# Last stage of a four-layer Flamingo block: values of two head pairs at a time, and other work moved between the slots

## The chip, the cores and the metric

The kernel runs on one core of one Trainium2 chip. The metric is device time in microseconds of one execution; three executions of the kernel before took 1777.65, 1778.09 and 1778.33 us, median 1778.09.

The engines of the core run side by side, each with its own instruction queue in order: TensorE (PE, matmuls; PEld are its weight loads), VectorE (DVE), ScalarE (ACT), GpSimd (POOL) and SyncE (SP, which here only issues DMAs). They meet through semaphores. Matmul results lie in PSUM[...].

## The reference

There are four layers on a batch of 16 sequences of 256 tokens, 256 channels each: a cross attention, a mixture of experts, a second cross attention, and a gated linear attention with a dense and a routed part. The change touches the last layer alone. Cut to what matters:

```python
q1 = (x @ Wq).reshape(B, L, H, DK) * scale;  k1 = (x @ Wk).reshape(B, L, H, DK)
v  = (x @ Wv).reshape(B, L, H, DV)
q2 = (x @ Wqa @ Wqb) * scale;  k2 = softmax(x @ Wka @ Wkb)          # per head
gk1 = log_sigmoid(x @ Wg1a @ Wg1b + bg1) / 16;  gk2 = ...           # decays
e = softmax(x @ We);  _, idx = top_k(e, 1);  mask = one_hot(idx)    # routing, 4 experts
o_dense  = gla(q1, k1, v, gk1)
o_sparse = sum over experts of gla(q2 * e * mask, k2 * e * mask, v, gk2 * mask)
o = o_dense + o_sparse
g = x @ Wga @ Wgb                                                    # output gate
o = o * rsqrt(mean(o * o) + EPS) * norm_w * (g * sigmoid(g))         # per head
x = x + tanh(g_ffn[1]) * (o.reshape(B, L, H * DV) @ Wo)
```

Here `x` is the normalised input (layer norm), H = 8 heads of 64, and `gla` is a causal linear attention with decays.

## The kernel before

`stage3_fast` computes the last layer. Its loop at the end runs over p = 4 b + m: b is the batch (0 to 15), m the pair of heads (0 to 3). I call the four steps of a batch its **slots 0 to 3**. All engines keep the program's order in this stage. What a slot does is written out in the loop, together with tables (`middle`, `rest`, `late`, `behind_factors`, `by_rows`, `logs`), which say by p % 4 which step runs at which place of the slot, and for which batch (an offset to b).

For each head pair, in this order through slots p-1 to p+1:

- `keys_queries` (bank `kq`): keys and queries, 4 matmuls, 8 records in the profile (each fp32 matmul gives two).
- `decays` (banks `gq`, `gz`): sums of the log gates along the tokens for the dense and the routed part, then four exps on ACT (`ee`).
- `factors` on DVE (`f`): keys and queries of the dense part times the exps. `second` and `factors_second`: keys and queries of the routed part (`k` on POOL, `q` on DVE).
- `products(p, 0)` and `products(p, 1)`: scores of the dense and the routed part (`sc`, `sc1`). The two heads of a pair lie in two row tiles of 64.
- `masked(p, 0)` (`at` on DVE), `masked(p, 1)` (four scalar_tensor_tensor instructions on DVE, then the sum of both parts by POOL's `at<-at,at`).
- `values`: the summed scores times `v`, into the bank `o`, two column tiles of 64. `summed(p)` calls it for p-1, and at even p also `squares` (ACT). `gated` multiplies `o` by the output gate `gw` into `u` (DVE).

Once for each batch:

- `lows` in slot 0 (the narrow projections), for the next batch. `all_gates` and `gates_end` in slot 1: exps of the gates into `lg`; `gate_logs` later turns them into logs.
- Routing: `route_logits`, `route_sums` and `route` (DVE, 32x32 tiles). `route` ends with SP's DMA `picks<-chosen` to memory and two DMAs back: `rows<-picks` (spread over the partitions) and `cols<-picks`. `same` (`em`) and `weights` (`am`), on DVE, build masks from both.
- Output gate: `outgates` in slot 0, `outgates_copy` (`zs`), and `outgates_end` for each of two halves: two ACT instructions on `eg`, then POOL's `gw<-zs,eg`.
- `stats`, `norm_ahead` (`xn`) and `turn_ahead` for the batch after next: the layer norm, and its transposition by DVE and by 16 SP DMAs `xnT<-turned`, which `lows` of that batch needs.
- `norms` in slot 1 for the batch before: sums of squares (bank `ms`), `rs` on ACT, SP's DMA `rms<-rs` to memory and two DMAs `r<-rms` back; `normed_out` (POOL, two `u<-u,r`), then `project` in slot 3: 16 records `proj<-wo,u`, the residual on DVE and the output DMA.

SP issues its DMAs in the program's order: in a batch `lowd`, `low`, then `picks`, `rows`, `cols`, `rms`, two `r`, sixteen `xnT`, `out`.

Tiles with the same tag share buffers in turn. In `f3w2` each tag has two. The tag `zs` serves both halves of the output gate and `rows`:

```python
x = w2.tile([P, 512], F32, tag="zs", name="rows") if b else ...     # route, line 1760
e, zs = (w2.tile([P, 512], F32, tag=n, name=n) for n in ("eg", "zs"))   # outgates
```

`bank(...)` gives one of two general PSUM banks in turn. `psa` is one pair of banks for scores (`sc`), also used by `all_gates`; `kq`, `gq`, `gz` and `o` have a bank each.

Of the kernel before, what the change touches and what calls it, by code (L numbers as in the profile page):

```python
# [10 lines left out]
F32 = mybir.dt.float32  # L11
I32 = mybir.dt.int32
AF = mybir.ActivationFunctionType
# [60 lines left out]
def layers(ctx: ExitStack, tc: tile.TileContext, t, out, check):  # L74
# [1559 lines left out]
    def stage3_fast(early_bank):  # L1634

        with ExitStack() as sx:
# [7 lines left out]
            def bank(name):  # L1644
                return pss.tile([P, 512], F32, tag="ps", name=name) if pss else early_bank(name)
# [129 lines left out]
            def all_gates(b):  # L1775

                lg[b] = of(b).tile([P, 2, 2, 512], F32, tag="lg", name="lg")
                two = psa.tile([P, 2, 512], F32, tag="sc", name="sc")
                one = [bank("z"), bank("z")]
                for i in (1, 0):  # L1780
                    for n, (lo, hi) in enumerate(((0, 17), (32, 49))):
                        x, w = (low2[lo:hi, :], lbg2[lo:hi, :]) if i else (low[b][64 + lo:64 + hi, 1, tokens(0)],
                                                                         lbg[64 + lo:64 + hi, :])
                        matmul(two[:, n, :] if i else one[n], x, w, start=True, stop=True)
                act3.activation(lg[b][:, 0, 0, :], one[0], AF.Exp, scale=-1.0)
                act3.activation(lg[b][:, 1], two, AF.Exp, scale=-1.0)
                z_[b, "z"] = one[1]

            def gates_end(b):
                act3.activation(lg[b][:, 0, 1, :], z_.pop((b, "z")), AF.Exp, scale=-1.0)  # L1790

            def gate_logs(b, i):
                act3.activation(lg[b][:, i], lg[b][:, i], AF.Ln, bias=1.0)
# [136 lines left out]
            def products(p, n):  # L1930

                b, m, cols = place(p)
                q, k = fq.pop((p, n)), fk.pop((p, n))
                if p == last - 1 and n == 1:
                    two = [psu.tile([P, 512], F32, tag=x, name="sc1") for x in ("kq", "gq")]
                elif n == 1 and m > 1:
                    two = [bank("sc1"), bank("sc1")]
                else:
                    ps = z_[p, n, "sc"] = psa.tile([P, 2, 512], F32, tag="sc", name="sc")
                    two = [ps[:, 0, :], ps[:, 1, :]]  # L1940
                for lo, hi, i in ((0, S, 0), (P, S, 1)):
                    for j in range(2):
                        r = slice(64 * j, 64 * j + 64)
                        matmul(two[j][:, lo + i * P:hi + i * P], k[r, tokens(i)], q[r, lo:hi],
                                         start=True, stop=True)
                if n == 1:
                    z_[p, n, "sc"] = two

            def masked(p, n):
                b, m, cols = place(p)  # L1950
                ps = z_.pop((p, n, "sc"))
                a = w2.tile([P, 2, 384], F32, tag=f"at{n}", name=f"at{n}")
                if n == 0:
                    at[p] = a
                    dve3.tensor_tensor(a, ps[:, :, :384], bc(amask, [P, 2, 384], 1), ALU.mult)
                else:
                    r = rd[b][:, 2 * m:2 * m + 2, :]
                    parts = [(j, 0, S, 0) for j in range(2)] + [(j, S, 3 * P, 1) for j in range(2)]
                    for j, lo, hi, i in parts if p == last - 1 else sorted(parts):
                        dve3.scalar_tensor_tensor(a[:, j, lo:hi], ps[j][:, lo:hi], r[:, i, j:j + 1],  # L1960
                                                  am[b][:, lo:hi], ALU.mult, ALU.mult)
                    if p == last - 1:
                        at[p, 1] = a
                        return
                    pool3.tensor_tensor(at[p], at[p], a, ALU.add)

            def values(p, first=True, end=True):
                b, m, cols = place(p)
# [13 lines left out]
            def squares(b, mp):  # L1982
                if mp == 0:
                    u_[b] = w2.tile([P, 4, S], F32, tag="u", name="u")
                    oT[b] = u_[b]
                    sq[b] = w2.tile([P, 4, S], F32, tag="sq", name="sq")
                ps = o.pop((b, mp))
                act3.activation(sq[b][:, 2 * mp:2 * mp + 2, :].rearrange("p m s -> p (m s)"), ps, AF.Square)
                z_[b, mp, "o"] = ps
# [17 lines left out]

            rms = [tc.dram_tile([8, S], F32, name=f"rms{b}") for b in range(B - 1)]

            def scaled_first(b):  # L2010
                if b == B - 1:
                    scaled(b, 0)

            def norms(b):

                if b == B - 1:
                    return
                ps, x = bank("ms"), sq.pop(b)
                for m in range(4):
                    matmul(ps[32 * m:32 * m + 32, :S], halves[:, 48:80], x[:, m, :], start=True, stop=True)  # L2020
                y = w2.tile([P, S], F32, tag="rs", name="rs")
                act3.activation(y, ps[:, :S], AF.Ln, bias=eps, scale=1.0 / 64, accum_out=check["logs"][:, 2 * b:2 * b + 1])
                act3.activation(y, y, AF.Exp, scale=-0.5)
                sp.dma_start(out=rms[b], in_=y[0:P:16, :])
                r = z_[b, "r"] = w1.tile([P, 4, S], F32, tag="r", name="r")
                for j in range(2):
                    sp.dma_start(out=r[64 * j:64 * j + 64],
                                      in_=bc(rms[b].rearrange("(m j) s -> j m s", j=2)[j], [64, 4, S], 0))
# [22 lines left out]
            def project_part(b, i, h):  # L2051
# [4 lines left out]
                if h == 1:  # L2056
# [1 line left out]
                                              ALU.mult, ALU.add)  # L2058
                    sp.dma_start(out=out[b, tokens(i)], in_=xs[b][:, i, :])

            start = {}
            middle = {0: [(lows, 1)], 1: [(outgates_end, 0, 0), (all_gates, 1)], 3: [(scaled_first, 0)]}

            rest = {0: [(bias, 2)], 1: [(route_sums, 1), (route, 1)],
                    2: [(norm_ahead, 2), (steepest, 1, 0)], 3: [(steepest, 1, 1)]}
            late = {0: [(shares, 0)], 1: [(norms, -1)], 2: [(vals, 1), (turn_ahead, 2)], 3: [(project, -1)]}
            behind_factors = {0: [(shares_end, 0)], 2: [(same, 1)]}
            by_rows = {0: [(outgates, 0), (route_logits, 1)], 1: [(gates_end, 1)]}
            logs = {0: [(outgates_copy, 0)],
                    1: [(stats, 2), (outgates_end, 0, 1), (gate_logs, 1, 0)],  # L2070
                    2: [(gate_logs, 1, 1), (normed_out, -1, 0), (normed_out, -1, 1)]}

            def run(steps, p):
                for f, d, *a in steps.get(p % 4, ()):
                    if 0 <= p // 4 + d < B:
                        f(p // 4 + d, *a)
# [3 lines left out]
            yield  # L2080
            for group in (((stats, 0),), ((norm, 0),), ((turn, 0),), ((lows, 0),), ((gates, 0, 0), (route_logits, 0)),
                          ((route_sums, 0), (route, 0)), ((gates, 0, 1), (gate_logs, 0, 0)),
                          ((vals, 0), (gate_logs, 0, 1), (stats, 1), (steepest, 0, 0), (same, 0))):
                for f, *a in group:
                    f(*a)
                yield
# [21 lines left out]

            dve3.tensor_scalar(wo, wo3, vec[:, V_NW:V_NW + 1], None, ALU.mult)
            def summed(p):  # L2110
                values(p - 1)
                if p % 2 == 0:
                    squares((p - 1) // 4, (p - 1) % 4 // 2)

            for p in range(last - 1):
                run(start, p)
                if 0 < p:
                    masked(p - 1, 1)
                if 1 < p and p % 2 == 1:
                    gated((p - 2) // 4, (p - 2) % 4 // 2)  # L2120
                keys_queries(p + 1)
                run(middle, p)
                run(rest, p)
                if p % 4 == 3 and p > 3:
                    weights(p // 4 + 1)
                decays(p + 1)
                run(late, p)
                ahead = p % 4 != 1 and p not in (3, last - 2)
                if ahead:
                    factors(p + 1)  # L2130
                    run(behind_factors, p)
                    if 0 < p:
                        summed(p)
                products(p, 0)
                masked(p, 0)
                if not ahead:
                    factors(p + 1)
                run(by_rows, p)
                if not ahead:
                    summed(p)  # L2140
                second(p + 1)
                factors_second(p + 1)
                if p == 3:
                    weights(1)
                run(logs, p)
                products(p, 1)

            b, p = B - 1, last - 1
            products(p, 0)
# [4 lines left out]
            masked(p, 1)  # L2154
            scaled(b, 0)
            project(b - 1, 0)
            summed(p)
            values(p, end=False)
            values(p, first=False)
            ends = Verdict()  # L2160
# [138 lines left out]
```

## Time and profile before

| | us |
|---|---|
| median of three executions | 1778.09 |
| profiled execution | 1777.46 |
| its span, first to last instruction | 1775.6 |
| last stage, TensorE from 1217.75 to 1769.0 | 551.25 |
| one batch of it, 1564.50 to 1598.97 | 34.47 |

Busy us of the engines in that batch, by slot (the window view):

| slot, from kq to kq | length | PE | DVE | ACT | POOL |
|---|---|---|---|---|---|
| 0 | 8.82 | 8.82 | 6.02 | 2.92 | 3.94 |
| 1 | 7.65 | 7.65 | 7.01 | 7.36 | 3.79 |
| 2 | 8.99 | 8.99 | 6.89 | 6.34 | 6.13 |
| 3 | 9.01 | 9.01 | 7.55 | 2.34 | 4.11 |

In the profile's lines L50 is the helper that nearly every instruction of DVE, ACT, POOL and SP goes through, and L1652 the helper of the matmuls, so groups are told apart by their tiles: `o<-at,v` is an instruction that writes `o` and reads `at` and `v`. Numbers of buffers are left out. An idle time in square brackets stands before the instruction, with what ended it. The granted TensorE clock was 1.00 of full speed through the stage.

### The profile page before, as it was taken

The numbers are of one execution on the slowest core, as the hardware profiler recorded it, in microseconds if no ns is written. First come the engines' busy times: TensorE is split into PE (matmuls) and PEld (weight loads), VectorE is DVE, ScalarE is ACT, GpSimd is POOL, SyncE is SP. The second block draws the span as 40 slices with busy tenths as digits, with TensorE's granted clock in tenths as the row PEclk, the third lists the DMA queues.
The fourth block names the chain that finished last, engine by engine and source line by source line (L and its number), as shares of the span: only waits on it lengthen the run. The fifth ranks groups of instructions, "written<-read, shape, count | busy, mean of one in ns | idle before, by whom it ended". The sixth has DMA issues, their size and how long they took to land.

```text
span 1775.6 us, 35325 instructions
## 1 busy us (share of the span) xinstructions
PE 1756.2 (99%) x13800; PEld 1223.8 (69%) x13800; DVE 1188.2 (67%) x2713; ACT 854.5 (48%) x1764; POOL 1019.1 (57%) x1002
## 2 busy tenths in 40 slices
PE   8999999999999999999999999999999999999998
PEld 5666666666666766666678776666777777777776
DVE  3345665656566656666557358888878778877876
ACT  4434443334433443344333357876546545645653
POOL 3655676577557666677562586622545545554553
PEclk9999999999999999999999999999999999999999
DMA  9800010100100010001017883300111211211111
GB/s 309 242 1 22 14 40 7 32 20 13 32 28 18 12 36 10 29 13 32 10 65 248 251 200 51 48 14 17 33 41 40 49 42 35 53 38 41 40 45 33
DMA packets 121625, 102.30 MB, mean 58 GB/s; under 512 B 53052, under 2 KB 106980, under 8 KB 120938
## 3 DMA queue, kind: packets, MB, share of 16 engines
q1 hardware_dynamic: 109161, 83.17, 16.2%
q0 software_dynamic: 12288, 16.79, 4.7%
q8 instruction: 111, 1.82, 0.4%
q14 instruction: 65, 0.52, 0.1%
HBM read 56.26 MB, written 38.44 MB: 53 GB/s over the span
## 4 chain that ended last, share of the span: by engine, by line
PE 86%; POOL 7%; DVE 3%; issue 2%; ACT 1%; DMA 0%; POOLq 0%; SPq 0%; DVEq 0%; ACTq 0%
PE o L50 12%; PE qk L50 11%; PE v L50 9%; PE sc L50 8%; PE proj L50 8%; PE kq L1652 7%; PE sc L1652 6%; POOL es L50 4%; PE gq L1652 3%; PE ex L50 3%; PE v L1652 3%; PE proj L1652 3%; PE o L1652 3%; PE gz L1652 2%; PE q L50 2%; POOL rs L50 2%
## 5 line engine op out<-in xcount | busy, mean ns | idle before, releaser
L50 POOL TENSOR_SCALAR rs<-mv 128x2 f32<-128x2 f32 (+2 forms) x85 | 16.2, 190 | 372.0 <-DVE mv L50 368.2
L50 DVE RECIPROCAL rd<-o 128x256 f32<-128x256 f32 x64 | 112.3, 1755 | 163.8 <-PE o L50 123.8
L50 POOL TENSOR_TENSOR at<-at,at 128x768 f32<-128x768 f32 x63 | 114.3, 1814 | 150.1 <-DVE at L50 150.1
L50 ACT ACTIVATE e<-sc 128x1024 f32<-128x1024 f32 (+1 forms) x192 | 181.5, 1015 | 18.5 <-PE sc L50 18.5
L50 PE MATMUL sc<-qk 64*128 64x256 f32 (+1 forms) x1536 | 183.1, 384 | 0.5 <-DVE qk L50 0.5
L50 PE MATMUL o<-e,v 128*32 128x256 f32 (+1 forms) x3072 | 177.9, 379 | 0.0
L50 PEld LDWEIGHTS sc<-qk 64*128 64x128 f32 (+1 forms) x1536 | 132.0, 172 | 55.1 <-issue 26.8
L50 POOL TENSOR_TENSOR esum<-esum,es 128x512 f32<-128x512 f32 x128 | 163.4, 1277 | 10.0
L50 PE MATMUL qk<-kvT,wkv 128*128 128x333 f32 x512 | 164.3, 443 | 0.0
L50 ACT ACTIVATE qk<-qk 128x256 f32<-128x256 f32 x128 | 48.7, 380 | 231.8 <-PE qk L50 231.8
L50 POOL TENSOR_TENSOR es<-e 128x1024 f32<-128x1024 f32 x64 | 151.3, 2364 | 12.0 <-ACT e L50 9.0
L50 POOL TENSOR_TENSOR es<-es,e 77x1024 f32<-77x1024 f32 x64 | 150.3, 2348 | 5.0
L50 PEld LDWEIGHTS o<-e,v 128*32 128x32 f32 (+1 forms) x3072 | 99.9, 110 | 66.3
L50 PE MATMUL qk<-kvT,wq 128*128 128x256 f32 x512 | 134.6, 385 | 0.0
L50 DVE COPY qk<-qk 128x333 f32<-128x333 f32 x128 | 64.6, 504 | 93.9 <-ACT qk L50 92.9
L50 POOL DMA_INDIRECT x<-rows_out,pos x64 | 101.0, 1578 | 33.7 <-issue 16.2
L50 PEld LDWEIGHTS qk<-kvT,wq 128*128 128x128 f32 x512 | 94.2, 189 | 35.2 <-issue 9.6
L50 PEld LDWEIGHTS qk<-kvT,wkv 128*128 128x128 f32 x512 | 97.2, 190 | 30.0
L50 PE MATMUL proj<-wo0h,oT 128*128 128x256 f32 x512 | 113.7, 380 | 0.3 <-DVE oT L50 0.3
L50 PE MATMUL v<-wkv,kvT 128*128 128x512 f32 x256 | 113.1, 595 | 0.0
L50 PEld LDWEIGHTS proj<-wo0h,oT 128*128 128x128 f32 x512 | 95.9, 190 | 13.9 <-issue 0.8
L50 POOL DMA_INDIRECT rows<-xw,pos x64 | 66.7, 1041 | 58.6 <-DMA rows<-xw,pos 26.4
(256 smaller groups left out, 3922.2 us busy)
## 6 DMA issues: line engine op xcount, KB each, us to landing
rows<-zero SPq DMA_DIRECT2D x16, 640.0 KB
xin<-rows SPq DMA_DIRECT2D x16, 640.0 KB
r<-rms SPq DMA_DIRECT2D x30, 256.0 KB
rows_out<-y SPq DMA_DIRECT2D x16, 384.0 KB
v<-vctx SPq DMA_DIRECT2D x15, 308.0 KB
x<-in_x_dram SPq DMA_DIRECT2D x16, 256.0 KB
rows_out<-y SPq DMA_DIRECT2D x16, 256.0 KB
rows<-picks SPq DMA_DIRECT2D x16, 256.0 KB
```

The costliest lines, as they stand in the source:

```text
L50: x = getattr(self.engine, name)(*a, **k)
L1652: tc.keep_in_program_order(nc.tensor.matmul(*a, **k))
```

## The change

`values` is called for two head pairs at a time, at even p. The routed scores of slot 1 move to the general banks and ahead of the `second` matmuls, and the POOL sums of slots 0 and 1 follow each other. The third exp of the gates joins `all_gates`. `norms` uses the bank `o`. Statistics and `norm_ahead` move to slot 0, `bias` to slot 3, `weights` to slot 2, both halves of `outgates_end` to slot 2, `gated` of a batch's first half to slot 3, both `steepest` to slot 3. `scaled_first`, which the loop never reached, goes.

```diff
                 act3.activation(lg[b][:, 1], two, AF.Exp, scale=-1.0)
-                z_[b, "z"] = one[1]
-
-            def gates_end(b):
-                act3.activation(lg[b][:, 0, 1, :], z_.pop((b, "z")), AF.Exp, scale=-1.0)
+                act3.activation(lg[b][:, 0, 1, :], one[1], AF.Exp, scale=-1.0)
...
-                elif n == 1 and m > 1:
+                elif n == 1 and m > 0:
                     two = [bank("sc1"), bank("sc1")]
...
-                    pool3.tensor_tensor(at[p], at[p], a, ALU.add)
+                    if m > 0:
+                        both(p, a)
+                    else:
+                        z_[p, "a"] = a
+
+            def both(p, a):
+                pool3.tensor_tensor(at[p], at[p], a, ALU.add)
...
-                ps, x = bank("ms"), sq.pop(b)
+                ps, x = psu.tile([P, 512], F32, tag="o", name="ms"), sq.pop(b)
...
-            middle = {0: [(lows, 1)], 1: [(outgates_end, 0, 0), (all_gates, 1)], 3: [(scaled_first, 0)]}
-
-            rest = {0: [(bias, 2)], 1: [(route_sums, 1), (route, 1)],
-                    2: [(norm_ahead, 2), (steepest, 1, 0)], 3: [(steepest, 1, 1)]}
-            late = {0: [(shares, 0)], 1: [(norms, -1)], 2: [(vals, 1), (turn_ahead, 2)], 3: [(project, -1)]}
-            behind_factors = {0: [(shares_end, 0)], 2: [(same, 1)]}
-            by_rows = {0: [(outgates, 0), (route_logits, 1)], 1: [(gates_end, 1)]}
-            logs = {0: [(outgates_copy, 0)],
-                    1: [(stats, 2), (outgates_end, 0, 1), (gate_logs, 1, 0)],
+            middle = {0: [(stats, 2), (lows, 1)], 1: [(all_gates, 1)], 2: [(outgates_end, 0, 0)]}
+
+            rest = {1: [(route_sums, 1), (route, 1)], 3: [(gated, 0, 0), (steepest, 1, 0), (bias, 3)]}
+            late = {0: [(shares, 0)], 1: [(norms, -1)], 2: [(vals, 1), (outgates_end, 0, 1), (turn_ahead, 2)],
+                    3: [(steepest, 1, 1), (project, -1)]}
+            behind_factors = {0: [(norm_ahead, 2), (shares_end, 0)], 2: [(same, 1), (weights, 1)]}
+            by_rows = {0: [(outgates, 0), (route_logits, 1)]}
+            logs = {0: [(outgates_copy, 0)], 1: [(gate_logs, 1, 0)],
                     2: [(gate_logs, 1, 1), (normed_out, -1, 0), (normed_out, -1, 1)]}
...
             def summed(p):
-                values(p - 1)
                 if p % 2 == 0:
+                    values(p - 2)
+                    values(p - 1)
                     squares((p - 1) // 4, (p - 1) % 4 // 2)
 
             for p in range(last - 1):
-                run(start, p)
                 if 0 < p:
                     masked(p - 1, 1)
-                if 1 < p and p % 2 == 1:
-                    gated((p - 2) // 4, (p - 2) % 4 // 2)
+                if 1 < p and p % 4 == 1:
+                    gated(p // 4 - 1, 1)
                 keys_queries(p + 1)
                 run(middle, p)
                 run(rest, p)
-                if p % 4 == 3 and p > 3:
-                    weights(p // 4 + 1)
                 decays(p + 1)
+                if p % 4 == 3:
+                    factors(p + 1)
                 run(late, p)
-                ahead = p % 4 != 1 and p not in (3, last - 2)
-                if ahead:
+                if p % 4 < 3:
                     factors(p + 1)
-                    run(behind_factors, p)
-                    if 0 < p:
-                        summed(p)
+                run(behind_factors, p)
+                if 0 < p:
+                    summed(p)
                 products(p, 0)
                 masked(p, 0)
-                if not ahead:
-                    factors(p + 1)
                 run(by_rows, p)
-                if not ahead:
-                    summed(p)
+                if p % 4 == 1:
+                    products(p, 1)
                 second(p + 1)
                 factors_second(p + 1)
-                if p == 3:
-                    weights(1)
+                if p % 4 == 1:
+                    both(p - 1, z_.pop((p - 1, "a")))
                 run(logs, p)
-                products(p, 1)
+                if p % 4 != 1:
+                    products(p, 1)
```

`bias` of batch 2 moves to the preparation in the stage before, and the last batch calls `values(p - 1)` where it called `summed(p)`.

## The prediction

> **What bounds the kernel now.** I read the busy shares first, then the stage alone, then the chain of waits over one batch, then the engines' timelines in the same window. The page's first part:
>
> ```profile
> PE 1756.2 (99%) x13800; PEld 1223.8 (69%) x13800; DVE 1188.2 (67%) x2713; ACT 854.5 (48%) x1764; POOL 1019.1 (57%) x1002
> ```
>
> [...]In the batch that I follow, slots 0 to 3 start with their kq matmuls at 1564.50, 1573.32, 1580.97 and 1589.96, and the next batch at 1598.97: 8.82 + 7.65 + 8.99 + 9.01 = 34.47 us. Parts of the chain of waits there (start, us, what):
>
> ```profile
> 1577.97 0.91 PE sc L1652 x8
> 1578.88 0.80 PE o L1652 x8
> 1579.68 0.41 PE gq L1652
> 1580.09 0.01 PE gz L1652
> 1580.10 0.21 PE gq L1652
> 1580.31 0.01 PE gz L1652
> 1580.31 0.65 PE sc L1652 x8
> ...
> 1592.77 3.46 PE proj L1652 x16
> 1596.23 0.80 PE o L1652 x8
> 1597.03 0.85 PE sc L1652 x8
> ```
>
> The chain is TensorE from end to end: in this stage only an uncovered matmul or a wait of TensorE costs time. A group that follows one of another shape costs extra: the second `sc` (0.65, behind matmuls of its own shape) against the first (0.85 to 0.91) though both have the same columns; `gq` 0.41 behind `o` against 0.21. But the page also shows a second chain, covered narrowly. SP's queue and POOL in the same batch:
>
> ```profile
> 1578.70 0.34 SPq L50 DMA_DIRECT2D picks<-chosen  x1
> 1580.09 0.34 SPq L50 DMA_DIRECT2D rows<-picks  x1
> 1580.49 0.43 SPq L50 DMA_DIRECT2D cols<-picks  x1
> 1581.00 0.60 SPq L50 DMA_DIRECT2D rms<-rs  x1
> 1583.86 1.33 SPq L50 DMA_DIRECT2D r<-rms  x2
> 1585.34 10.33 SPq L50 DMA_DIRECT2D xnT<-turned  x16
> ```
>
> ```profile
> 1576.68 1.28 POOL L50 TENSOR_TENSOR gw<-zs,eg 128x512 f32<-128x512 f32 x1
> ...
> 1588.88 2.51 POOL L50 TENSOR_TENSOR u<-u,r 128x512 f32<-128x512 f32 x2 [1.73 <-DMA r<-rms]
> ```
>
> SP issues in order, so `rms`, `r` and the 16 `xnT` DMAs stand behind `rows`. From the start of `rows`: `rms` +0.91, `r` +3.77, landing (POOL's start) +8.79, first half of `u` done +10.04 (1.25 each), second +11.30. The projection needs both: it starts at 1592.77.
>
> **The change, part by part.** Let S be the start of slot 1's kq; times below are us after S.
>
> *Values in pairs.* No matmul goes or comes. Slot 1 loses `o` (0.80), and its `gq` no longer follows another shape (0.64 for the four pieces becomes 0.44): 7.65 - 1.00 = 6.65. Slot 3 loses `o` (0.80); `sc` then follows `proj` directly, and where it follows 128x128 matmuls (last batch, 1753.38) it took 0.85, as now: 8.21. Slots 0 and 2 each gain a second `o` behind one of its own shape. No row shows that; with the columns of `sc` I take 0.65, bounds 0.64 and 0.80: 9.47 and 9.64. Sum 33.97, so 0.50 us less per batch, some 7.5 us in all, if nothing waits.
>
> *All three gate exps in one place.* The third `lg` exp (0.58) moves ahead of the `ee` exps on ACT. TensorE's gates still end about 3.0, the exps start at 3.07, 3.56, 4.47, so `ee` of gq starts at 4.96 rather than 4.47 and ends at 5.63. Queued behind: `ee` of gz (POOL's `k` can start at 5.9), `rs`, `e2`. TensorE's second scores want their second bank, freed by that exp at 5.05, at 5.53: covered. `gq` and `gz` want theirs at 6.2; `ee` of gz ends at 6.2: nothing, at most 0.1.
>
> *Statistics and normalisation to slot 0.* Four bn instructions (1.0) go into DVE's wait for `low` (2 us there), two `xn` exps (1.09) ahead of `sq` on ACT, which waits for the longer `o` anyway: nothing. `bias` moves by a slot on POOL, which has idle time (18.0 busy of 34.5): nothing. `norms` taking the `o` bank waits for `u` at 2.0, needed at 4.07: nothing.
>
> *Weights to slot 2* (four `am`, 2.05 on DVE): slot 2's 1.70 of idle takes most, slot 3 loses them. No cost by itself.
>
> *Output gates to slots 2 and 3.* Here is the wait. `rows` is a tile under the tag `zs`, of two buffers; the two `zs` of the batch take both, so `rows` gets the first one's buffer, and in the built program SP's `rows` DMA waits for POOL's first `gw`, before and after. Before, that `gw` ends at 1577.96, ahead of `picks`, and the wait is free. After, `outgates_end` for it runs in slot 2, and POOL's order is k, add of slot 0, add of slot 1, gw, gw, k, u, u. Forward: DVE's `f` waits for `ee` until 5.7, then by start distances of this batch `at` 6.3, `q` 7.17, second masks 7.5 to 8.86; the add of slot 0 runs 6.6 to 8.4; the add of slot 1 starts 0.14 behind the masks, at 9.0; 1.77 later `gw` starts, and ends at 12.05. The exps of `eg` are ready by 9.5 and do not decide.
>
> So `rows` starts at 12.1, where it stood at 6.77. Everything queued behind it on SP follows: `r` lands at 20.9, `u` is done at 22.14 and 23.40. TensorE reaches `proj` at 6.65 + 9.64 + 2.81 = 19.10. It waits for the first half and its weights (0.25) until 22.4, does two products (0.86), waits for the second half to 23.65, and has six left (2.60): end 26.25 against 22.56, a loss of 3.69. Said as a threshold: `rows` may start at 8.4 without harm, and each us after that costs a us.
>
> Other followers of `rows`: `em` and `am` on DVE. With landing of `rows` near 16.2 (r's own 4.2 from its second issue), `q` of slot 2 ends about 20.5, and slot 3's `gq` waits for its bank from 18.2 to 20.6; that lies inside the wait for `u` and adds nothing. The last `xnT` issue ends at 12.1 + 15.58 = 27.7; `low` wants them at 30.1. Their landing is not shown; the nearest row is picks to rows (1.39 from issue to the next start), so about 29.2: nothing. If they land as `r` does (4.2), 31.3 and 1.2 more.
>
> New period: 6.65 + 9.64 + (8.21 + 3.69) + 9.47 = 37.66, that is +3.19. Fourteen batches have `rows` and a projection in the loop: 44.7. Batch 0 has `rows` but no projection; there `q` of slot 2, the two `gates` and `f` on DVE run late and `low` comes about 2.9 later. The last batch has no `rows`; its edits about cancel. Sum +47.6 on the profiled execution's 1777.46 (span 1775.6 and 1.9 around it): 1825. Its time is 0.6 below the median shown, less than the sum's error.
>
> **Two rules against the rows.** (1) DVE's `e<-e,eden` took 0.94 and `eq<-e,choice` 0.99 while POOL added, and the same shape 0.18 with POOL idle. The Trainium skill, "SBUF — State Buffer", section "Who interferes with whom", says that a VectorE instruction with two SBUF inputs stands behind a GpSimd instruction that reads SBUF until that ends. After the change POOL is idle beside this chain, so by the rule `picks` comes 1.6 earlier; by the rows kept as they are it does not. If `rows` still waited for `picks` that would bring it forward; as it waits for `gw`, both give 1825. (2) A rule that speaks against long holes: "TensorE: Matmul & The Clock Gate", Part 1, has the array fall to half clock after an idle window of about 3.4 us. In this stage no TensorE wait exceeds 0.6 and the granted clock is 1.00 throughout. The new holes are about 2.4 (for `gq`), 0.9 and 0.4 us with work between; by the row the clock stays and the time is 1825; by the rule, should a window lie in a hole, a window at half clock costs some 1.7 us in each of 14 batches, an estimate of 1849. I take the row.
>
> **Rivals.** *The wait is harmless, 1770*: only TensorE's 0.50 per batch shows. For it: TensorE is the whole chain today. Against: `gw` would have to end by 8.4, when POOL has only just finished the first add. *Faster ends and slower ends part at `rows` = 8.9*, where the stall eats the 0.50. *Part of it, about 1800*: were POOL's adds or DVE's masks earlier; the earliest `gw` end I can build (masks right behind the scores at 6.2, so adds back to back) is 11.5, still +2.6 per batch, 1816. *Worse, about 1847*: the `xnT` landing or the clock on top.
>
> **How the numbers follow.** Main case 0.76, own range 1814 to 1836 (`gw` end 11.5 to 12.8); part of it 0.07; worse 0.09; harmless 0.06; 0.02 for a cancelling near zero. The range takes in the main case and reaches towards both neighbours: 1803 to 1843. A difference under 0.2% (3.6 us) cannot be told from no change. Faster 0.06, same 0.02, slower 0.92.
>
> **What would show it.** Right: `rows` starts about 12 us after slot 1's kq, directly behind `gw`; POOL's `u` waits for `r` until about 21; the waits list has TensorE's `proj` waiting for POOL `u`, some 3 us fourteen times; slot 1 lasts 6.7 us; the batch 37.7. Wrong: a batch of 34.0 with no TensorE wait (the pairing alone), or `rows` behind `picks` as today; `low` waiting for DMA, or a granted clock under 1.00, would mean the worse case.

## The result, and the profile after

The kernel after takes 1831.97 us (median of five, 1828.12 to 1833.06) against 1777.79 us of the kernel before (1777.65 to 1778.33): a ratio of 1.030, 95% interval 1.0289 to 1.0311. Its profiled execution spans 1831.3 us. The engines' counts of instructions are those of before, and TensorE is busy for only 13.2 us more in a span that is 55.7 us longer; the page's first part and the chain's shares:

```profile
PE 1769.4 (97%) x13800; PEld 1228.6 (67%) x13800; DVE 1155.2 (63%) x2713; ACT 853.2 (47%) x1764; POOL 1017.8 (56%) x1002
...
PE 74%; POOL 10%; DMA 6%; DVE 5%; issue 3%; ACT 1%; SPq 1%; POOLq 0%; DVEq 0%; ACTq 0%
```

A batch from about the same time as the one shown before starts its slot 1 at S = 1569.51. The next kq groups start at 1576.44, 1586.09 and 1597.56, and slot 0 had started at 1560.11. The slots are thus 9.40, 6.93, 9.65 and 11.47, together 37.45 us against 34.47. SP's queue in this batch (start, length, what):

```profile
1573.39 0.34 SPq L50 DMA_DIRECT2D picks<-chosen  x1
1581.58 0.35 SPq L50 DMA_DIRECT2D rows<-picks  x1
...
1582.50 0.62 SPq L50 DMA_DIRECT2D rms<-rs  x1
1585.44 1.33 SPq L50 DMA_DIRECT2D r<-rms  x2
```

`picks` leaves at S+3.88 and `rows` only at S+12.07: 8.2 us between two DMAs that were 1.39 apart before. The chain of waits, followed back from slot 3's projection (start, length, what), shows the cause:

```profile
1578.51 1.82 POOL at L50
1580.33 1.23 POOL gw L50
...
1581.58 0.35 SPq L50
...
1582.50 2.88 DMA rms<-rs
...
1586.15 4.00 DMA r<-rms
...
1591.51 1.28 POOL u L50
...
1592.83 2.86 PE proj L1652 x12
```

POOL adds the scores of slot 1, then makes `gw`; 0.02 later SP issues `rows` (x1 below tests that the shared buffer makes it wait). The normalisation DMAs follow in the queue, and TensorE waits for them. Its timeline in slot 3 (the idle time in brackets stands before the instruction):

```profile
1589.63 0.71 PE L1652 MATMUL gq<-dmask,lg 128*128 128x128 f32 x4 [1.55 <-DVE q L50]
...
1591.61 4.08 PE L1652 MATMUL proj<-wo,u 128*128 128x256 f32 x16 [0.81 <-POOL u L50]
```

There are two holes, 1.55 behind DVE's `q` and 0.81 behind POOL's `u`. The projection takes 4.08 where the kernel before, and x1 below with `u` early, show 3.62: another 0.46 inside the group is waiting for the second half of `u`.

One thing that was only in my worse case is in the windows view (stretch, its length, then busy us of PE, PEld, DVE, ACT and POOL, granted clock, DMA share, GB/s):

```profile
1325.00:1332.00 7.00, 6.17 (x26) 4.71 (x28) 3.89 (x5) 0.46 (x2) 5.68 (x5) 0.76 0.17 26
...
1706.20:1713.00 6.80, 6.72 (x18) 5.20 (x20) 1.12 (x2) 0.00 (x0) 4.91 (x5) 0.57 0.16 24
```

In these two and one more of the fourteen batches the granted clock fell behind the holes, and the projections there took 5.43, 6.58 and 5.22 us against 4.09 elsewhere, 5.0 us more in all.

### The profile page after: what moved, and what is told of

Same layout as the page of the kernel before. It is cut to its first block, busy times and chain, and to the rows that moved or that the text cites. A ratio compares the mean times of both kernels' runs of the same rounds, so it can differ in the third digit from the quotient of the medians.

```text
span 1831.3 us, 35342 instructions
## 1 busy us (share of the span) xinstructions
PE 1769.4 (97%) x13800; PEld 1228.6 (67%) x13800; DVE 1155.2 (63%) x2713; ACT 853.2 (47%) x1764; POOL 1017.8 (56%) x1002
## 3 DMA queue, kind: packets, MB, share of 16 engines
q8 instruction: 111, 1.82, 0.4%
## 4 chain that ended last, share of the span: by engine, by line
PE 74%; POOL 10%; DMA 6%; DVE 5%; issue 3%; ACT 1%; SPq 1%; POOLq 0%; DVEq 0%; ACTq 0%
PE o L50 11%; PE qk L50 11%; PE v L50 9%; PE sc L50 8%; PE proj L50 7%; PE sc L1652 5%; PE kq L1652 4%; POOL es L50 4%; DMA r<-rms 3%; PE ex L50 3%; PE proj L1652 3%; DMA rms<-rs 2%; PE gq L1652 2%; DVE at L50 2%; PE low L1652 2%
## 5 line engine op out<-in xcount | busy, mean ns | idle before, releaser
L50 POOL TENSOR_TENSOR es<-e 128x1024 f32<-128x1024 f32 x64 | 151.2, 2362 | 12.1 <-ACT e L50 9.0
L50 POOL TENSOR_TENSOR k<-e,ee 128x256 f32<-128x256 f32 x64 | 47.5, 742 | 127.9 <-ACT ee L50 124.0
```

Of the source, the lines that this page charges most:

```text
L50: x = getattr(self.engine, name)(*a, **k)
```

## The experiments

Medians, and ratios to runs of the kernel before on the same chip. The slots are those of a typical batch.

| run | what differs | us | ratio, 95% interval | slots 0 to 3 |
|---|---|---|---|---|
| x1 | after, `rows` in an idle buffer | 1773.32 | 0.9977, 0.9967 to 0.9986 | 9.40 6.93 9.64 8.21 |
| x2 | after, first half of the gates back in slot 1 | 1772.94 | 0.9975, 0.9965 to 0.9985 | 9.40 6.93 9.65 8.21 |
| x9 | after, that half at the end of slot 1 | 1798.93 | 1.0118, 1.0102 to 1.0133 | 9.40 6.93 9.64 9.79 |
| x5 | after, `rows` behind `r` on SP | 1861.92 | 1.0469, 1.0453 to 1.0485 | 9.40 6.93 9.64 14.8 |
| x11 | x5, `u<-u,r` on DVE | 1809.09 | 1.0173, 1.0157 to 1.0189 | 9.40 6.93 9.64 10.03 |
| x3 | before, both halves of the gates in slot 2 | 1868.17 | 1.0517, 1.0501 to 1.0533 | 8.82 7.65 8.99 15.3 |
| x4 | before, values in pairs | 1787.06 | 1.0053, 1.0039 to 1.0067 | 9.47 7.71 9.64 8.21 |
| x6 | after, TensorE kept busy in the holes | 1827.10 | 1.0280, 1.0265 to 1.0296 | 9.40 6.93 9.64 11.5 |
| x7 | x1, decays ahead of the gates | 1779.34 | 1.0010, 1.0001 to 1.0019 | 9.40 7.32 9.64 8.21 |
| x8 | before, `rows` in an idle buffer | 1777.82 | 0.9999, 0.9990 to 1.0009 | 8.82 7.65 8.99 9.01 |
| x12 | x1, third exp of slot 1 left out | 1768.99 | 0.9949, 0.9936 to 0.9963 | 9.40 6.65 9.64 8.21 |
| x13 | x1, early keys in the bank of `ms` | 1768.46 | 0.9954, 0.9941 to 0.9968 | 9.40 6.65 9.64 8.21 |

### x1 and x8: the shared buffer

```diff
-                x = w2.tile([P, 512], F32, tag="zs", name="rows") if b else ...
+                x = w2.tile([P, 4, S], F32, tag="sq", name="rows")[:, :2, :].rearrange("p x s -> p (x s)") if b else ...
```

> The kernel after, with rows laid into an idle buffer (the tag sq, whose second buffer nothing uses) instead of the buffer of the first zs; every instruction and its order stay. Theory (the rows DMA waits for POOL's first gw only because both share a buffer): rows starts at S+5.2, 1.35 behind picks at S+3.85, TensorE waits neither for q nor for u, the batch is 6.93+9.64+8.21+9.40 = 34.2 us, and the time 1771 to 1777, about 1773.5. Rival A (the moved gates crowd POOL and ACT in slots 2 and 3, whatever buffer rows has): u is late behind gw, the batch stays over 36.5 us, the time over 1805. Rival B (pairs of values cost by themselves): slots 0 and 2 stay longer than forecast and the time lies over 1780.

> The kernel before, with rows in the idle buffer of sq. Theory (gw ends ahead of picks there, so that the shared buffer costs nothing): no change, 1776.5 to 1779. Rival (the shared buffer holds rows back in the kernel before, too): faster by 2 us or more.

The edit moves one tile and leaves every instruction in its place. In the kernel after it takes 58.7 us off (1831.97 to 1773.32), in the kernel before nothing (1777.82). SP's queue in x1, in the batch with S = 1502.19:

```profile
1506.08 0.34 SPq L50 DMA_DIRECT2D picks<-chosen  x1
1508.11 0.34 SPq L50 DMA_DIRECT2D rows<-picks  x1
```

`rows` starts at S+5.92 here, in most batches at 5.22 (5.2 was forecast), and slot 3 is 8.21 us in every batch with a projection. The whole loss was the wait for the buffer; what remains of the change is a small gain. In the kernel before the shared buffer was free early enough, as the prediction had it.

### x2, x9 and x3: where the gate stands

```diff
x2
-            middle = {..., 1: [(all_gates, 1)], 2: [(outgates_end, 0, 0)]}
+            middle = {..., 1: [(outgates_end, 0, 0), (all_gates, 1)]}
x9
-            middle = {..., 1: [(all_gates, 1)], 2: [(outgates_end, 0, 0)]}
+            middle = {..., 1: [(all_gates, 1)]}
-            logs = {0: [(outgates_copy, 0)], 1: [(gate_logs, 1, 0)],
+            logs = {0: [(outgates_copy, 0)], 1: [(outgates_end, 0, 0), (gate_logs, 1, 0)],
x3, on the kernel before
-            middle = {0: [(lows, 1)], 1: [(outgates_end, 0, 0), (all_gates, 1)], 3: [(scaled_first, 0)]}
+            middle = {0: [(lows, 1)], 1: [(all_gates, 1)], 2: [(outgates_end, 0, 0)], 3: [(scaled_first, 0)]}
-            late = {..., 2: [(vals, 1), (turn_ahead, 2)], 3: [(project, -1)]}
+            late = {..., 2: [(vals, 1), (outgates_end, 0, 1), (turn_ahead, 2)], 3: [(project, -1)]}
-                    1: [(stats, 2), (outgates_end, 0, 1), (gate_logs, 1, 0)],
+                    1: [(stats, 2), (gate_logs, 1, 0)],
```

> The kernel after, with the first half of outgates_end back in slot 1, ahead of all_gates, where it was before; rows keeps the shared buffer. Theory: gw ends before picks, so the shared buffer is free in time, rows starts at about S+5.2, batch 34.2 us, time about 1773.5 (1770 to 1777). Rival A (the second half of the gates, still in slot 2, is what is late): only part comes back, over 1790. Rival B (the pairs of values): over 1780.

> The kernel after, with the first half of outgates_end at the end of slot 1 (ahead of gate_logs), so that POOL's gw comes between its adds of slots 0 and 1: a middle dose of the delay. Theory: gw ends and rows starts at S+9.9 to 10.1 (12.0 in the kernel after, threshold 8.4 by the prediction, 8.7 with the slot 1 of 6.93 that was measured); gq no longer waits for q; the projection waits about 0.9 to 1.3 us per batch; batch 35.0 to 35.5; time 1784 to 1794. If the loss were a step and not in proportion to the delay (rival): 1773 or over 1820.

> The kernel before with one thing of the change: both halves of outgates_end moved to slot 2; values, gates, statistics stay. Theory: the moved gates alone make the loss. POOL's gw comes behind its add of slot 1 and ends at S+12.5 to 13, rows follows it, and by the threshold (here about 8.8) each us after it costs one: 3.7 to 4.3 per batch, 1827 to 1840, about 1834. Rival (the loss needs the pairs or the other moves): under 1800.

x2 came out as forecast: the first half of the gates (two ACT instructions and POOL's `gw`) earlier in the program, and everything is back, though the second half stays in slot 2.

x9 gives the middle dose. There `rows` starts at S+10.12 or 10.13; in the batch with S = 1482.36, SP and then TensorE:

```profile
1492.49 0.34 SPq L50 DMA_DIRECT2D rows<-picks  x1
```

```profile
1502.90 4.08 PE L1652 MATMUL proj<-wo,u 128*128 128x256 f32 x16 [0.66 <-POOL u L50]
```

Over the thirteen batches in which the clock did not fall, slot 3 takes 9.85 us on average; in the kernel after it takes 11.64 over eleven such batches, with `rows` at 12.07. Against 8.21 that is a loss of 1.64 and of 3.43. It so grows by 0.92 us for each us that `rows` is later, and the line through both reaches zero near 8.4: the prediction's threshold, and nearly its slope of one. Two doses always lie on a line; x1 is the third, with `rows` at 5.21 to 6.56 and no loss. In time x9 was 5 us above what I wrote: I had put the batch at 35.0 to 35.5, with 9.85 it is 35.8, and in one the clock fell (a projection of 5.61 us).

x3 shows that the moved gate alone, without pairs, makes the loss, and a larger one than forecast: `gw` ends at S+13.2, and behind it the holes were 0.66 (`gq`) and 3.38 us (`proj`) in the batch with S = 1587.86, about the 4 forecast:

```profile
1611.68 5.94 PE L1652 MATMUL proj<-wo,u 128*128 128x256 f32 x16 [3.38 <-POOL u L50]
```

On top of them the clock fell in twelve of the fourteen batches: this projection took 5.94 us, and the twelve 5.3 to 6.5. That is some 23 us over 4.09 each, of the 90 that x3 loses: the clock, which I had put at nothing, counts here.

### x6: is it the clock?

```diff
-                decays(p + 1)
+                decays(p + 1, 3 * (p % 4 == 3))
...
+                for _ in range(fill):
+                    matmul(gz[p][:, :D], ident, wo[:, 0, :], start=True, stop=True)
...
+                if part is None:
+                    matmul(ps[:, :D], ident, wo[:, 0, :], start=True, stop=True)
```

> The kernel after, with four extra matmuls of 128x256 per batch in slot 3 whose results are overwritten: three in the hole ahead of gq, one in the hole ahead of the projection, to keep TensorE busy there. The rows wait stays. Theory of the clock (the projections of 5.2 to 6.6 us are the half clock behind the holes, about 5 us in all): granted clock 1.00 in the whole stage, every projection of 16 records 4.1 us, time 1824 to 1829. Rival (those projections are slow because u or its weights come late): still some over 5 us and a time of 1831 to 1836, the extra work partly on the path.

The whole stage ran at full clock, and the fourteen projections took 4.08 or 4.09 us each; 1827.10 us is 4.9 below the kernel after. The intervals of the two ratios overlap, so the time alone would not decide it; the windows view of the stage, with the clock as the third number from its end, and the projection of the batch that was slowest in the kernel after do:

```profile
1240.00:1760.00 520.00, 507.25 (x3431) 372.73 (x3431) 352.62 (x829) 257.62 (x592) 241.14 (x243) 1.00 0.16 38
```

```profile
1701.97 4.08 PE L1652 MATMUL proj<-wo,u 128*128 128x256 f32 x16 [0.70 <-POOL u L50]
```

The projection still waits for `u` here, but is not slow. So the three long projections were the clock, set off by the holes, and not late data.

### x5 and x11: two followers of `rows`

```diff
x5
-                sp.dma_start(out=rows[b], in_=bc(picks[b], [P, 2, S], 0))
...
+            def fetch(b):
+                sp.dma_start(out=rows[b], in_=bc(picks[b], [P, 2, S], 0))
+                sp.dma_start(out=cols_[b], in_=picks[b].rearrange("n (i p) -> p n i", p=P))
...
-            late = {0: [(shares, 0)], 1: [(norms, -1)], ...
+            late = {0: [(shares, 0)], 1: [(norms, -1), (fetch, 1)], ...
x11, on top
-                    pool3.tensor_tensor(x, x, r, ALU.mult)
+                    dve3.tensor_tensor(x, x, r, ALU.mult)
...
-            behind_factors = {..., 2: [(same, 1), (weights, 1)]}
+            behind_factors = {..., 2: [(normed_out, -1, 0), (normed_out, -1, 1), (same, 1), (weights, 1)]}
-                    2: [(gate_logs, 1, 1), (normed_out, -1, 0), (normed_out, -1, 1)]}
+                    2: [(gate_logs, 1, 1)]}
```

> The kernel after, with the two DMAs rows and cols issued behind rms and the two r on SP, so that r no longer stands behind the wait for gw; rows itself still waits for it. This parts the two followers of rows: r, u, proj on one side, em, am, q, gq on the other. Theory of the prediction (the wait of gq for q lies inside the wait for u): with u early the gq wait of 1.55 us per batch is left alone and bounds, batch about 35.7 to 36.4, time 1795 to 1808. If r alone made the loss: about 1773. If rows by way of em and q made all of it: over 1820.

x5 was a miss by more than 50 us. `r` came early as planned, and no projection waited for `u` any more; but the early `u` now lay on POOL beside `em` and `am` on DVE. DVE and POOL of x5, in the batch with S = 1587.72:

```profile
1604.94 1.48 DVE L50 SCALAR_TENSOR_TENSOR am<-rows,cols 128x256 f32<-128x256 f32 x1
1606.46 1.36 DVE L50 SCALAR_TENSOR_TENSOR am<-am,cols,amask 128x256 f32<-128x256 f32 x1
1607.75 0.34 DVE L50 SCALAR_TENSOR_TENSOR am<-rows,cols 128x128 f32<-128x128 f32 x1
```

```profile
1604.83 2.71 POOL L50 TENSOR_TENSOR u<-u,r 128x512 f32<-128x512 f32 x2
```

Two `am` stand behind the two `u`; the third starts after POOL has ended at 1607.54 and takes 0.34. In the kernel after the same four `am` took 0.47, 0.48, 0.35 and 0.35, because `u` was late. `q` stands behind `am` on DVE, and `gq` waited 3.44 us for it; then the clock fell as well (5.2 to 5.8 us for twelve of the fourteen projections). x11 tests this reading:

> The run x5 (rows and cols behind r on SP, rows still waiting for gw) with the two u<-u,r on DVE ahead of em instead of on POOL. In x5 POOL's u (1604.83 to 1607.54) lay beside DVE's am, whose first two instructions took 1.48 and 1.36 us there against 0.47 and 0.48 in the kernel after. Theory (x5 was slower than forecast because POOL's u holds up DVE's instructions with two inputs in SBUF): with u off POOL, am takes 0.35 to 0.5 each again, q ends at about S+20.1, gq waits 1.5 to 1.9 us, the projection not at all; slot 3 about 9.9 us against 13.3 to 14.9 in x5, clock 1.00, time 1793 to 1804. Rival (am was late for another reason, the landing of rows or cols): slot 3 stays over 12 us, time over 1830.

With `u` on DVE the two instructions are short again, in all fourteen batches:

```profile
1611.08 0.47 DVE L50 SCALAR_TENSOR_TENSOR am<-rows,cols 128x256 f32<-128x256 f32 x1
1611.59 0.48 DVE L50 SCALAR_TENSOR_TENSOR am<-am,cols,amask 128x256 f32<-128x256 f32 x1
```

Slot 3 is 10.03 to 10.13 us in twelve of the fourteen batches; `gq` waits 1.55 to 1.65 us there, and a projection without any wait takes 3.62. In the other two (12.4 and 12.7 us) `r` landed later, so that the second `u<-u,r` lay beside POOL's `gw` and took 1.68 us instead of 0.60; `gq` waited 2.24 and 2.53 us, the clock fell, and the projections took 5.31. That puts the time 5 us above the forecast. What follows: `rows` has two followers. In the kernel after the one by `r` and `u` decides, and the one by `em`, `am` and `q` is hidden inside it. Alone it costs 1.82 us per batch (10.03 against 8.21), so that taking the first away leaves at least that.

### x4: the pairs alone

```diff
             def summed(p):
-                values(p - 1)
                 if p % 2 == 0:
+                    values(p - 2)
+                    values(p - 1)
```

> The kernel before with the other thing alone: values of two pairs at a time. Theory: it saves 0.50 us of TensorE per batch by fewer changes of shape, but slot 1's second scores keep the banks psa here, which DVE empties late once no group of values stands between the two: up to 0.45 per batch comes back. 1770 to 1778, about 1774. Rival (pairs cost by themselves, by squares or by buffers held longer): over 1782.

Outside the expected range, and 9.3 us slower than before. (In the last batch `values(p - 1)` stands for `summed(p)`.) Slots 0, 2 and 3 are 9.47, 9.64 and 8.21, to the hundredth what the prediction put down for the pairs. Slot 1 however grew to 7.71 where 6.65 was the hope; its part of the chain of waits:

```profile
1584.67 0.93 PE sc L1652 x8
...
1585.70 0.97 DVE at L50
...
1586.80 0.92 PE sc L1652 x8
```

Without a group of values between them, the second scores stand directly behind the first and wait for the same two banks until DVE has emptied them. So the pairs want the other half of the edit, the second scores in the general banks: in the kernel after, which has both, slot 1 is 6.93. No run has the pairs and this half without the rest, so that this half alone would do is argued from the chain, not shown.

### x7, x12 and x13: the 0.28 us of slot 1

Slot 1 came out at 6.93, not 6.65. In the kernel after, TensorE at its end:

```profile
1575.63 0.38 PE L1652 MATMUL gq<-low,lbk 64*128 64x256 f32 x1
1575.82 0.48 PE L1652 MATMUL gz<-low,lbk 64*128 64x256 f32 x1
1575.85 0.38 PE L1652 MATMUL gq<-low,lbk 64*128 64x256 f32 x1
1576.14 0.38 PE L1652 MATMUL gz<-low,lbk 64*128 64x256 f32 x1
```

Elsewhere the two run side by side, 0.01 apart; here `gz` is 0.19 and 0.29 late. ACT's `ee<-gz` read that bank until 1575.77. Three runs went after it:

```diff
x7, on x1
-            middle = {..., 1: [(all_gates, 1)], 2: [(outgates_end, 0, 0)]}
+            middle = {..., 2: [(outgates_end, 0, 0)]}
-            late = {0: [(shares, 0)], 1: [(norms, -1)], ...
+            late = {0: [(shares, 0)], 1: [(all_gates, 1), (norms, -1)], ...
x12, on x1
-                act3.activation(lg[b][:, 0, 1, :], one[1], AF.Exp, scale=-1.0)
...
+                dve3.tensor_scalar(lg[b][:, 0, 1, :], z_.pop((b, "z")), 0.0, None, ALU.max)
x13, on x1
-                    keys_ahead(*((b + 1, m - 1) if m else (b, 3)), gz[p][:, S:])
+                    ps = z_[b - 1, "ms"][0] if m == 2 and b > 0 else gz[p]
+                    keys_ahead(*((b + 1, m - 1) if m else (b, 3)), ps[:, S:])
...
-            logs = {0: [(outgates_copy, 0)], 1: [(gate_logs, 1, 0)],
+            logs = {0: [(outgates_copy, 0)], 1: [(norms_end, -1), (gate_logs, 1, 0)],
```

In x7 the exp of the pair of banks also comes first of the three; in x13 `norms_end` is the ACT and DMA part of `norms`.

> The kernel after with rows in an idle buffer (as in the run x1), and in slot 1 the decays of the next pair ahead of all_gates, with the exp of the two banks of sc first: ee no longer stands behind the three gate exps on ACT. Theory (the third exp costs slot 1 the 0.28 us by which it is longer than forecast, through ee of gz): slot 1 falls from 6.93 to 6.65 to 6.75, the time by 3 to 4 us from 1773.3 to about 1770. Rival (the 0.28 is a change of shape on TensorE, no wait): slot 1 stays 6.93 and the time 1773.

> The run x1 with the third gate exp of slot 1 taken off ACT: in its place DVE writes max(z, 0), so that exp is left out of the computation. Theory (slot 1 takes 6.93 and not 6.65 because the third exp puts ee of gz 0.5 later on ACT): slot 1 6.65, other slots unchanged, time 1768 to 1771. Rival (the 0.28 is a change of shape on TensorE): slot 1 6.93, time 1773.

> The run x1 (rows in an idle buffer) with all work kept, and in slot 1 the early keys of the next batch (the second-part matmul otherwise written into gz) laid into the free half of the bank of ms; the two rs instructions follow the exp of these keys on ACT. Nothing in slot 1 then waits for ee of gz. Theory (the run x12 showed 0.28 us per batch behind the third exp, and the wait is the bank gz): slot 1 6.65, other slots unchanged, time 1768 to 1771, the complete computation. Rival (the bank of ms is held longer, by rs, and another matmul waits for it, or gq is as late as gz was): slot 1 6.9 or more, 1773 or more.

x7 failed: with `ee` ahead of them the gate exps were late, and the first scores, which want the banks `psa`, waited 1.01 us for `lg` in the chain; slot 1 grew to 7.32. x12, which leaves the third exp out (DVE writes a maximum in its place), gave 6.65 to the hundredth and took 4.3 us off x1. So the 0.28 is the third exp on ACT's queue and no change of shape. x13 gives the same without leaving anything out: the matmul that waited for `gz` writes the free half of another bank. TensorE there:

```profile
1505.11 0.38 PE L1652 MATMUL gq<-low,lbk 64*128 64x256 f32 x1
1505.11 0.38 PE L1652 MATMUL ms<-low,lbk 64*128 64x256 f32 x1
```

At 1768.46 us (ratio 0.9954) x13 is faster than both kernels: the change without its wait, and without the 0.28.

## Why the prediction was right, and where it was off

The forecast was 1825 us by a wait of `rows` for `gw`; 1831.97 was measured, for that reason. Its steps, in us after S where they are places in the batch:

| step | predicted | measured |
|---|---|---|
| slots 0, 1, 2 | 9.47, 6.65, 9.64 | 9.40, 6.93, 9.65 |
| `rows` starts | 12.1 | 12.07 |
| `r` lands, `u` starts | 20.9 | 20.77 |
| `u` complete | 23.40 | 23.28 |
| projection complete | 26.25 | 26.18 |
| stall in slot 3 | 3.69 | 3.26 |
| batch | 37.66 | 37.45 |

- **The wait and its place: right.** x1, x2 and x3 show the cause from three sides: another buffer, another place of the gate, and the moved gate alone. x9 confirms the threshold.
- **The sum: 7 us short, by two errors that in part cancel.** It was put down as -7.0 for fourteen batches of pairing, +51.7 for the stalls and +2.9 for batch 0, in all +47.6. Measured are -4.2 (x1 against before) and, in the profiled execution, +55.0 (fourteen slots 3, 169.98 less 14 times 8.21), +3.1 (slot 3 of batch 0 and slot 0 after it against those of x1: 2.15 and 0.96) and +1.3 (three slots 0 of 9.68, 9.80 and 9.99 against 9.40, whose cause stays open). That makes 55.2, and this execution took 55.3 us more than the median before; the medians differ by 54.2. Of the 55.0, the wait as I meant it is 48.0, fourteen times the average of 3.43; I had put it 3.7 too high. The three batches with a fall of the clock add 7.0, which I had put at nothing: 5.0 in the projections, and most of the rest in one batch where `u` started only at S+22.62.
- **The third exp: mis-sized.** It was priced at "nothing, at most 0.1" because `ee` of gz would end at 6.2, just when `gz` is wanted. It ended at 6.26, TensorE arrived at 6.12, and the second matmul of the pair fell behind as well: 0.28. x12 measures it.
- **The clock: the wrong side taken.** I took the row (1.00 throughout) over the rule of the Trainium skill, "TensorE: Matmul & The Clock Gate", Part 1, since none of my holes was as long as its window of about 3.4 us. But the stage's trace of before had no holes of this size, so it could not speak about them. Here the clock fell in 3 of 14 batches, with holes of 1.55 to 1.62 and 1.2 to 2.6 us and 1.2 us of work between; nor did it fall in all fourteen, as my 1849 assumed. It cost 5.0 us in the profiled execution; x6, where it never fell, takes 4.9 less by the medians.
- **`em` and `am`: right here, too comfortable.** `gq` waited for `q` until 20.12 (20.6 was forecast), inside the wait for `u`. "Adds nothing" holds for this kernel only: x11 shows at least 1.55 us of wait there once `u` is out of the way, and x5 more.
- **The first rule: it held, and changed nothing.** The route chain came 1.5 us earlier (`picks` at S+3.88 against 5.38), as the rule had it and the rows kept as they were did not. By both readings that gains nothing, as `rows` waits for `gw` anyway. One reading of the prediction was inexact: before, `eq<-e,choice` stood beside POOL's `gw`, not beside an add.
- **The pairing: right in three slots**, and by the chain of x4 its fourth rests on the general banks. I had given the saving to the pairs alone.

## What to carry to other kernels

Before a step is moved later, ask for each buffer that it reads who takes that buffer next: here a POOL multiplication went 7.4 us later (its end from S+4.64 to S+12.04), and a DMA that shares nothing with it but the tag of its tile went with it, and a whole queue behind the DMA. A wait in a queue usually has several followers, so count the second one too before paying for the removal of the first. A trace without holes says nothing about what the clock does in holes; and holes must be added up, not taken one by one.

## What the runs showed of the hardware that I had not expected

**Half clock from short holes.** No single idle time of TensorE in this stage of the kernel after reached 3.4 us; the longest was 2.59. Yet projections took 5.2 to 6.6 us instead of 4.09, in some batches and not in others with nearly equal holes (1.55 and 1.18 us in one that fell; 1.55 and 1.21 in one that did not). The granted clock of the trace fell to one half at 1326.40, 1705.28 and 1746.24, for 3.41, 6.83 and 3.41 us, and these falls are 111 and 12 times 3.413 us apart. So it changes on a fixed grid, which fits a window that runs on by itself, as the Trainium skill, "TensorE: Matmul & The Clock Gate", Part 1, has it. The first three lines are the windows of this grid ahead of the falls, the fourth is a window that no fall followed (the first number behind the comma is TensorE's busy time):

```profile
1322.99:1326.40 3.41, 1.73 (x11) 1.48 (x12) 3.41 (x9) 1.21 (x4) 1.89 (x2) 1.00 0.31 48
1701.87:1705.28 3.41, 1.16 (x8) 0.97 (x8) 3.41 (x8) 1.21 (x4) 0.32 (x1) 1.00 0.72 155
1742.83:1746.24 3.41, 1.16 (x8) 0.97 (x8) 3.41 (x9) 1.21 (x4) 0.99 (x1) 1.00 0.47 101
1360.53:1363.95 3.41, 1.73 (x11) 1.13 (x9) 3.38 (x10) 0.54 (x2) 0.25 (x1) 1.00 0.58 144
```

TensorE was idle for 1.69, 2.26 and 2.26 us of them, and for 1.69 in the last. The kernel after, x3, x5, x9 and x11 have 33 falls in this stage. Each follows a window with 1.69 to 2.88 us idle, and at full clock no window with more than 1.74 us idle passed without a fall; x6, without a fall, has at most 1.19. In these runs, then, about half of a window was enough, in one piece or several, where the page asks for an idle window; the measurement decides. How the holes lie to the grid decides, and the grid lies differently in each execution.

**POOL holding DVE.** The Trainium skill, "SBUF — State Buffer", section "Who interferes with whom", has a VectorE instruction with two SBUF inputs contend with a GpSimd instruction that reads SBUF, over ports that only one can hold. The rows agree: `am` above; the two instructions of the route chain, in the kernel before beside POOL and then in the kernel after with POOL idle,

```profile
1575.83 0.94 DVE L50 TENSOR_TENSOR e<-e,eden 32x32 f32<-32x32 f32 x1
...
1577.02 0.99 DVE L50 TENSOR_TENSOR eq<-e,choice 32x32 f32<-32x32 f32 x1
```

```profile
1572.09 0.18 DVE L50 TENSOR_TENSOR e<-e,eden 32x32 f32<-32x32 f32 x1
...
1572.52 0.18 DVE L50 TENSOR_TENSOR eq<-e,choice 32x32 f32<-32x32 f32 x1
```

and in x2 the small `eq<-eq,prio`, which took 0.18 us in x1 with POOL idle and 1.20 beside the `gw` that had been moved back:

```profile
1504.95 1.20 DVE L50 TENSOR_TENSOR eq<-eq,prio 32x32 f32<-32x32 f32 x1
```

```profile
1504.83 1.28 POOL L50 TENSOR_TENSOR gw<-zs,eg 128x512 f32<-128x512 f32 x1 [5.02 <-ACT eg L50]
```

I had not expected that it would turn the removal of a wait into a loss of 30 us, as in x5. It does not do so alone: behind the longer hole of 3.44 us the clock fell, and x5's fourteen projections took some 24 us over 3.62 each.
